# A two-product attention kernel: the second product turned round to 512 moving columns, with the running sum of the exponentials made by accumulating DMAs

## Chip, cores, metric

One core of one Trainium2 chip. The metric is the device time of one execution in microseconds (us), as the median of several runs. All runs told of here are of the fast state. A ratio is the mean time of one kernel's fast runs over the mean of the kernel before in the same rounds, so it is not quite the ratio of the medians that are quoted.

## The reference

Self-attention over 4 images of 64 x 64 positions, 256 channels, with 128-channel queries and keys, all in float32:

```python
q = x @ Wq + bq;  k = x @ Wk + bk;  v = x @ Wv + bv      # 4096 positions an image
pq, pk, pv = (t.reshape(B, -1, N) for t in (q, k, v))     # N = 4096: a reshape, not a transpose
energy = einsum('bcn,bcm->bnm', pq, pk)
attention = softmax(energy, axis=-1)
out = einsum('bcm,bnm->bcn', pv, attention).reshape(x.shape)
return gamma * out + x
```

## The kernel before

The energies of an image, 4096 x 4096, are never stored. For a group of queries the kernel walks over the keys in units: the first product (f32) gives energies in PSUM, ScalarE takes their exponentials, and the second product adds exponentials times v to accumulators. The second product keeps f32 accuracy from faster fp32r matmuls: each operand is given in three forms h, l and d (an upper part, the rest, and a difference), and three matmuls stand for one. A group has 256 queries, a unit has 4 key blocks of 128. The exponentials stand still as stationary operand, 128 queries at a time, and v's forms move. vh and vl carry two extra columns of ones, so that the softmax's denominator comes out of the same accumulation as column 256.

```python
NB = 256                                # queries a group; 64 groups, 8 units each
def energy(b, u):                       # first product, exp, upper part
    ...
    nc.tensor.matmul(sp[:, i, :], pr.pk[:, ...], pr.pqf[:, g * NB : (g + 1) * NB], ...)
    nc.scalar.activation(x[:, 2 * k : 2 * k + 2, :], sp, AF.Exp)
    ...
    nc.scalar.activation(h, x, AF.Identity, scale=UPPER)

def halves(b, u):                       # l = x - h, d = (1 + E) h - x, on VectorE
    ...

def attend(b, u):                       # second product, 24 matmuls a unit
    for j in range(NJ):                 # 2 halves of the queries
        a, bb = now["acc"][j]
        for i in range(4):
            for out_, left, right, ... in ((a, h, vh, ...), (a, l, vl, ...), (bb, d, vd, ...)):
                nc.tensor.matmul(out_, left[:, i, n], right[:, m, :], ...)

def finish(b, g, acc):                  # 1/z, combine a and bb, transpose back, add x, store
    ...

for u in range(STEPS):                  # the order on every engine's queue
    if u + LOOK < STEPS: energy(b, u + LOOK)      # LOOK = 2
    proceed()                           # one more piece of a finish that is under way
    if u + 1 < STEPS: halves(b, u + 1)
    attend(b, u)
    proceed()
```

Of the kernel before, what the change touches and what calls it, by code (L numbers as in the profile page):

```python
# [18 lines left out]
def kernel(  # L19
# [12 lines left out]

# [24 lines left out]
    P = 128  # L57
# [114 lines left out]

    NB = 256
    NJ = NB // P
    NG = N // NB
    NU = NM // 4
    STEPS = NG * NU
    LOOK = 2
    LAG = 3
# [7 lines left out]
    zall = const.tile([P, B * NG, NJ], F32, name="zall")  # L187
# [3 lines left out]
    with ExitStack() as fast:  # L191
# [5 lines left out]
        ppool, work = pool("ppool", 2), pool("work", 2)  # L197
# [4 lines left out]
        vh = qkv.tile([P, NM, C + 2], F32R, tag="vh", name="vh")  # L202
        vl = qkv.tile([P, NM, C + 2], F32R, tag="vl", name="vl")
        vd = qkv.tile([P, NM, C], F32R, tag="vd", name="vd")
        for t in (vh, vl):
            nc.vector.tensor_copy(t[:, :, C:], ones[:, : 2 * NM].rearrange("p (m t) -> p m t", t=2))

        images, units, now = [], {}, {}
# [11 lines left out]
        def image(b):  # L220
            def xt_out(i):
                return xtpool.tile([P, KC, 2, P], F32, tag="xt", name=f"xts_{b}_{i}")

            def v_out(i):
                now["v4"] = work.tile([P, KC, C], F32, tag="v4", name=f"v4_{b}_{i}")
                return now["v4"], bv4_sb, 1.0 / E

            images.append(Projection(b, xpool, qkv, (ps_s, "s"), xt_out, v_out))

        def project_v(b, i):  # L230
            images[b].v(i)
            v4 = now["v4"]
            m = slice(2 * i, 2 * i + 2)
            h = vh[:, m, :C]
            nc.scalar.activation(h, v4, AF.Identity, scale=UPPER * E)  # L235

            for t, f in ((vl, 1.0 / E), (vd, 1.0 / E + 1.0)):
                nc.vector.scalar_tensor_tensor(  # L238
                    t[:, m, :C], h.bitcast(F32), -f, v4, ALU.mult, ALU.add
                )  # L240

        def energy(b, u):

            g, t = divmod(u, NU)
            pr = images[b]
            x = ppool.tile([P, 4, NB], F32, tag="x", name=f"x_{b}_{u}")
            for k in range(2):
                sp = ps_s.tile([P, 2, NB], F32, tag="s", name=f"s_{b}_{u}_{k}")
                for i in range(2):
                    nc.tensor.matmul(  # L250
                        sp[:, i, :],
                        pr.pk[:, 4 * t + 2 * k + i, :],
                        pr.pqf[:, g * NB : (g + 1) * NB],
                        start=True,
                        stop=True,
                    )
                nc.scalar.activation(x[:, 2 * k : 2 * k + 2, :], sp, AF.Exp)  # L257
            h = ppool.tile([P, 4, NB], F32R, tag="h", name=f"h_{b}_{u}", bufs=LOOK + 1)
            nc.scalar.activation(h, x, AF.Identity, scale=UPPER)  # L259
            units[b, u] = x, h  # L260

        def halves(b, u):
            x, h = units[b, u]
            l = ppool.tile([P, 4, NB], F32R, tag="l", name=f"l_{b}_{u}")
            nc.vector.tensor_tensor(l, x, h.bitcast(F32), ALU.subtract)  # L265

            d = ppool.tile([P, 4, NB], F32R, tag="d", name=f"d_{b}_{u}")
# [3 lines left out]
            units[b, u] = h, l, d  # L271

        def attend(b, u):
            g, t = divmod(u, NU)
            if t == 0:
                now["acc"] = [
                    (
                        ps_o.tile([P, C + 2], F32, tag=f"a{j}", name=f"a{j}_{b}_{g}"),
                        ps_o.tile([P, C], F32, tag=f"b{j}", name=f"b{j}_{b}_{g}"),
                    )  # L280
                    for j in range(NJ)
                ]
            h, l, d = units[b, u]
            for j in range(NJ):
                a, bb = now["acc"][j]
                for i in range(4):
                    m = 4 * t + i
                    n = slice(j * P, (j + 1) * P)
                    for out_, left, right, first, last in (
                        (a, h, vh, True, False),  # L290
                        (a, l, vl, False, True),
                        (bb, d, vd, True, True),
                    ):
                        nc.tensor.matmul(  # L294
                            out_,
                            left[:, i, n],
                            right[:, m, :],
# [3 lines left out]
            if t == NU - 1:  # L301
                start(finish(b, g, now["acc"]))

        def finish(b, g, acc):
            xr = load_x(xpool, b, g)
            z = zall[:, b * NG + g, :]
            r = work.tile([P, 2, NJ], F32, tag="r", name=f"r_{b}_{g}")
            o = work.tile([P, NJ, C], F32, tag="o", name=f"o_{b}_{g}")
            for j in range(NJ):
                a, bb = acc[j]  # L310
                nc.vector.tensor_copy(z[:, j : j + 1], a[:, C : C + 1])
                nc.vector.reciprocal(r[:, 0, j : j + 1], z[:, j : j + 1])
                nc.vector.tensor_tensor(  # L313
                    r[:, 0, j : j + 1], r[:, 0, j : j + 1], gam, ALU.mult
                )
                nc.vector.tensor_scalar(
                    r[:, 1, j : j + 1], r[:, 0, j : j + 1], 1.0 + E, None, ALU.mult
                )
                nc.scalar.activation(  # L319
                    o[:, j, :], bb, AF.Identity, scale=r[:, 0, j : j + 1]  # L320
                )
                nc.vector.scalar_tensor_tensor(  # L322
                    o[:, j, :], a[:, :C], r[:, 1, j : j + 1], o[:, j, :], ALU.mult, ALU.add
                )
            yield
            yield
            tp = ps_s.tile([P, 2, NB], F32, tag="s", name=f"ot_{b}_{g}")
            for s in range(2):
                for j in range(NJ):
                    nc.tensor.transpose(  # L330
                        tp[:, s, j * P : (j + 1) * P], o[:, j, s * P : (s + 1) * P], ident
                    )
            nc.vector.tensor_tensor(xr, xr, tp, ALU.add)  # L333
            nc.gpsimd.dma_start(ov[b, g], xr)  # L334

        for b in range(B):
# [15 lines left out]
            halves(b, 0)  # L352
            for u in range(STEPS):
# [3 lines left out]
                if u + 1 < STEPS:  # L357
                    halves(b, u + 1)
# [7 lines left out]
    zf = zall.rearrange("p n j -> p (n j)")  # L366
    nc.vector.tensor_reduce(zs[:, 0:1], zf, AX.X, ALU.min)
    nc.vector.tensor_reduce(zs[:, 1:2], zf, AX.X, ALU.max)
    nc.vector.tensor_scalar(zs[:, 0:1], zs[:, 0:1], Z_LOW, None, ALU.is_lt)
    nc.vector.tensor_scalar(zs[:, 1:2], zs[:, 1:2], Z_HIGH, None, ALU.is_gt)  # L370
    nc.vector.tensor_tensor(zs[:, 0:1], zs[:, 0:1], zs[:, 1:2], ALU.add)
    with tc.tile_pool(name="ps_z", bufs=1, space=PSUM) as ps_z:
        zp = ps_z.tile([P, 1], F32, name="zp")
        nc.tensor.matmul(zp, ones, zs[:, 0:1], start=True, stop=True)
        nc.vector.tensor_copy(again, zp)

    NB = 512
    NG = N // NB
    NJ = NB // P
    NP = NM // 2  # L380
# [127 lines left out]
```

## Time and profile before

| | kernel before |
|---|---|
| median, range | 2666.5 us, 2664.6 to 2667.2 (3 runs) |
| TensorE, VectorE, ScalarE, GpSimd busy | 99%, 57%, 50%, 2% |
| granted TensorE clock | 0.999 |

The busy shares, the chain, the groups and the timeline of a group's end stand in the prediction below, with how to read them. Here is only what the waits of this kernel say (engine, line and tile that waited, for whom, us in total, times, longest):

```profile
ACT x L257 <- PE s L250: 1042.6, 880, 2.6
DVE l L265 <- issue: 841.8, 380, 2.6
PE a L294 <- DVE l L265: 1.9, 4, 0.5
```

ScalarE waits for TensorE's energies. VectorE waits too, with no other engine named (its buffers come free when TensorE is done with them). TensorE's own waits for VectorE are small: 1.9 us in the line above, and 3.0 us for d in the group lines of the prediction. The kernel is bound by TensorE.

### The profile page before, as it was taken

The page shows a single profiled execution, that of the slowest core. Times are in us where ns is not written, and L with a number is a line of the kernel's source. Part 1 is how long each engine was busy: PE and PEld are TensorE (multiplying, and loading weights), DVE is VectorE, ACT ScalarE, POOL GpSimd, SP SyncE. Part 2 cuts the span into 40 slices and gives each one's busy share as a digit, 9 for nine tenths or more (in the row PEclk, how much of TensorE's full clock was granted, in tenths as well). Part 3 has the DMA queues.
Part 4 walks back from the last instruction along what each step waited for, and adds up shares of the span by engine and source line. Part 5 has one row for each costly group of instructions (what it writes and reads, how often), then busy time and mean ns, then how long its engine had stood idle before and what let it go on. Part 6 is the DMA issues. An engine that isn't in the chain of part 4 may idle for free.

```text
span 2665.1 us, 42006 instructions
## 1 busy us (share of the span) xinstructions
PE 2639.4 (99%) x17922; PEld 2486.4 (93%) x17922; DVE 1506.8 (57%) x1993; ACT 1333.7 (50%) x1922; POOL 44.8 (2%) x70
## 2 busy tenths in 40 slices
PE   8999999999999999999999999999999999999998
PEld 7999999999899999999989999999998999999998
DVE  3555555555465555555545555555555555555555
ACT  3555555455455455455445555455545555545543
POOL 0000000000000000000000000000000000000000
PEclk9999999999999999999999999999999999999999
DMA  2000000000200000000020000000002000000000
GB/s 89 9 16 10 17 17 17 13 13 17 72 9 17 13 13 16 17 17 9 17 72 9 17 17 9 17 17 17 17 17 64 9 17 17 17 9 17 17 9 10
DMA packets 41667, 53.76 MB, mean 20 GB/s; under 512 B 3584, under 2 KB 37376, under 8 KB 41472
## 3 DMA queue, kind: packets, MB, share of 16 engines
q1 hardware_dynamic: 34816, 33.56, 4.1%
q0 software_dynamic: 5120, 16.78, 1.8%
q8 instruction: 142, 2.33, 0.3%
q10 hardware_dynamic: 1536, 0.66, 0.1%
q14 instruction: 53, 0.43, 0.0%
HBM read 34.21 MB, written 16.78 MB: 19 GB/s over the span
## 4 chain that ended last, share of the span: by engine, by line
PE 98%; DVE 1%; ACT 0%; DMA 0%; issue 0%; POOL 0%; ACTq 0%
PE a L294 37%; PE s L250 33%; PE b L294 18%; PE qk L136 4%; PE v L156 4%; PE ot L330 1%; PE xt L123 1%; DMA bv_sb<-in_L_conv_bv_dram 0%; DVE d L268 0%; DVE l L265 0%; ACT v L165 0%; ACT o L319 0%; DMA wqk_sb<-in_L_conv_Wk_dram 0%; DVE vl L238 0%; ACT vh L235 0%; DVE o L322 0%
## 5 line engine op out<-in xcount | busy, mean ns | idle before, releaser
L294 PE MATMUL a<-vh,h 128*128 128x258 f32 x4096 | 1242.3, 303 | 0.0
L294 PE MATMUL a<-vl,l 128*128 128x258 f32 x4096 | 1156.2, 282 | 1.9 <-DVE l L265 1.9
L294 PE MATMUL b<-vd,d 128*128 128x256 f32 x4096 | 1151.3, 281 | 3.0 <-DVE d L268 3.0
L257 ACT ACTIVATE x<-s 128x512 f32<-128x512 f32 x1024 | 610.5, 597 | 1056.2 <-PE s L250 1042.6
L265 DVE TENSOR_TENSOR l<-x,h 128x1024 fp32r<-128x1024 f32 x512 | 626.5, 1224 | 844.4 <-issue 841.8
L250 PE MATMUL s<-pq,pk 128*128 128x256 f32 x4096 | 966.5, 379 | 0.0
L250 PEld LDWEIGHTS s<-pq,pk 128*128 128x128 f32 x4096 | 741.2, 190 | 80.3
L294 PEld LDWEIGHTS a<-vl,l 128*128 128x128 f32 x4096 | 773.1, 189 | 14.5 <-DVE l L265 3.1
L294 PEld LDWEIGHTS a<-vh,h 128*128 128x128 f32 x4096 | 773.6, 189 | 11.5
L294 PEld LDWEIGHTS b<-vd,d 128*128 128x128 f32 x4096 | 774.0, 189 | 3.8 <-DVE d L268 3.8
L268 DVE SCALAR_TENSOR_TENSOR d<-h,x 128x1024 fp32r<-128x1024 f32 x512 | 623.9, 1219 | 0.0
L259 ACT ACTIVATE h<-x 128x1024 fp32r<-128x1024 f32 x512 | 542.7, 1060 | 16.3
L136 PE MATMUL qk<-wqk_sb,xts 128*128 128x256 f32 x512 | 123.5, 385 | 7.7 <-ACT xts L129 7.7
L156 PE MATMUL v<-xts,wv_sb 128*128 128x256 f32 x512 | 119.7, 379 | 0.0
L319 ACT ACTIVATE o<-b,r 128x256 f32<-128x256 f32 x128 | 60.6, 474 | 108.2 <-DVE r L313 108.2
L136 PEld LDWEIGHTS qk<-wqk_sb,xts 128*128 128x128 f32 x512 | 93.9, 193 | 19.4 <-ACT xts L129 8.8
L156 PEld LDWEIGHTS v<-xts,wv_sb 128*128 128x128 f32 x512 | 97.3, 190 | 13.2
L238 DVE SCALAR_TENSOR_TENSOR vl<-vh,v 128x512 fp32r<-128x512 f32 x64 | 44.4, 693 | 113.1 <-ACT vh L235 113.1
L165 ACT ACTIVATE v<-v,bv_sb 128x256 f32<-128x256 f32 x128 | 53.6, 469 | 105.6 <-PE v L156 105.6
L322 DVE SCALAR_TENSOR_TENSOR o<-a,r,o 128x256 f32<-128x256 f32 x128 | 62.0, 484 | 52.6 <-ACT o L319 52.6
L334 POOL DMA_DIRECT2D out_dram<-x x64 | 44.1, 690 | 2613.3 <-DVE x L333 2575.5
L333 DVE TENSOR_TENSOR x<-x,ot 128x512 f32<-128x512 f32 x64 | 44.0, 687 | 39.1 <-PE ot L330 39.1
(32 smaller groups left out, 406.1 us busy)
## 6 DMA issues: line engine op xcount, KB each, us to landing
x<-in_x_dram SPq DMA_DIRECT2D x128, 256.0 KB, 2.9
out_dram<-x POOLq DMA_DIRECT2D x64, 256.0 KB, 2.5
wv_sb<-in_L_conv_Wv_dram ACTq DMA_DIRECT2D x1, 256.0 KB, 4.4
wqk_sb<-in_L_conv_Wq_dram ACTq DMA_DIRECT2D x1, 128.0 KB, 2.1
wqk_sb<-in_L_conv_Wk_dram ACTq DMA_DIRECT2D x1, 128.0 KB, 3.1
bqk_sb<-in_L_conv_bq_dram ACTq DMA_DIRECT2D x1, 64.0 KB, 5.5
bqk_sb<-in_L_conv_bk_dram ACTq DMA_DIRECT2D x1, 64.0 KB, 5.8
bv_sb<-in_L_conv_bv_dram ACTq DMA_DIRECT2D x2, 0.5 KB, 5.1
```

The source lines that it names most:

```text
L136: nc.tensor.matmul(qk[:, s, :], self.xt[i][:, k, s, :], wqk_sb[:, k, :], start=(k == 0), stop=(k == KC - 1),)
L156: nc.tensor.matmul(vp[:, eh, :], wv_sb[:, k, eh * P : (eh + 1) * P], self.xt[i][:, k].rearrange("p s a -> p (s a)"), start=(k == 0), stop= ...
L165: nc.scalar.activation(to[:, eh, :], vp[:, eh, :], AF.Identity, bias=bias[:, eh : eh + 1], scale=scale,)
L238: nc.vector.scalar_tensor_tensor(t[:, m, :C], h.bitcast(F32), -f, v4, ALU.mult, ALU.add)
L250: nc.tensor.matmul(sp[:, i, :], pr.pk[:, 4 * t + 2 * k + i, :], pr.pqf[:, g * NB : (g + 1) * NB], start=True, stop=True,)
L257: nc.scalar.activation(x[:, 2 * k : 2 * k + 2, :], sp, AF.Exp)
L259: nc.scalar.activation(h, x, AF.Identity, scale=UPPER)
L265: nc.vector.tensor_tensor(l, x, h.bitcast(F32), ALU.subtract)
L268: nc.vector.scalar_tensor_tensor(d, h.bitcast(F32), 1.0 + E, x, ALU.mult, ALU.subtract)
L294: nc.tensor.matmul(out_, left[:, i, n], right[:, m, :], start=(m == 0 and first), stop=(m == NM - 1 and last),)
L319: nc.scalar.activation(o[:, j, :], bb, AF.Identity, scale=r[:, 0, j : j + 1])
L322: nc.vector.scalar_tensor_tensor(o[:, j, :], a[:, :C], r[:, 1, j : j + 1], o[:, j, :], ALU.mult, ALU.add)
```

## The change

The intent: let v's forms stand still and the exponentials move, 512 at a time, so that the number of second-product matmuls halves. The output then comes out with channels on partitions, which is the layout of the result, so the transposes at a group's end go. But a column sum of the exponentials is no longer a by-product: there are no columns of ones any more. It is made by DMAs that add each pair's exponentials to a tile in SBUF, off every engine's path, and at the group's end one f32 product with ones sums it over the partitions.

```diff
-    NB = 256
+    NB = 512            # 32 groups of 512 queries, 16 pairs of key blocks each
-    LAG = 3
+    LAG = 1
-        vh = qkv.tile([P, NM, C + 2], F32R, tag="vh", name="vh")      # likewise vl; vd without ones
+        vh, vl, vd = (qkv.tile([P, NM, C], F32R, ...) for f in "hld")
...
+        def forms(b, u):                # was halves(): l and d as before, and
+            if t == 0:
+                now["sum"] = work.tile([P, 2, NB], F32, tag="sum", ..., bufs=2)
+                nc.gpsimd.dma_start(now["sum"], x)
+            else:
+                nc.gpsimd.dma_start(now["sum"], x, accum_op=ALU.add)
...
         def attend(b, u):
-                        nc.tensor.matmul(out_, left[:, i, n], right[:, m, :], ...)
+                    for s in range(2):  # 12 matmuls a pair
+                        nc.tensor.matmul(to[s], left[:, m, s * P : (s + 1) * P], right[:, i, :], ...)
...
+        def finish(b, g, acc, total):   # in pieces; each yield is one proceed()
+            for s in range(2):
+                nc.scalar.copy(o[:, s, :], bb[s])
+                nc.vector.scalar_tensor_tensor(o[:, s, :], aa[s], 1.0 + E, o[:, s, :], ...)
+            yield
+            nc.vector.tensor_tensor(z, total[:, 0, :], total[:, 1, :], ALU.add)
+            yield
+            nc.tensor.matmul(zb, ones, z, start=True, stop=True)
+            nc.scalar.activation(z, zb, AF.Identity, accum_out=...)
+            yield
+            ...                         # two half reciprocals, scale by 1/z and gamma, add x, store
```

A unit is now a pair of key blocks with 512 queries: the same number of exponentials as a unit before. There are 512 units in both kernels. Not shown in the cut: x gets three buffers instead of two, x for the residual comes in two loads a group, and the check of the denominators' range at the end is written anew.

More of the change, by code (lines that the diff above doesn't have):

```diff
@@ L171, in v @@
                 )
-    NB = 256
-    NJ = NB // P
+    NB = 512
+    HB = NB // 2
     NG = N // NB
-    NU = NM // 4
-    STEPS = NG * NU
+    NP = NM // 2
+    STEPS = NG * NP
     LOOK = 2
-    LAG = 3
+    LAG = 1
     E = 2.0**-12
@@ L185 @@
     again = const.tile([P, 1], I32, name="again")
-    zall = const.tile([P, B * NG, NJ], F32, name="zall")
+    zsum = const.tile([P, 2, B * NG], F32, name="zsum")
     bv4_sb = const.tile([P, KC], F32, name="bv4_sb")
@@ L196 @@
         xpool, xtpool, qkv = pool("xpool", 4), pool("xtpool", LAG + 2), pool("qkv", 1)
-        ppool, work = pool("ppool", 2), pool("work", 2)
+        ppool, work = pool("ppool", 2), pool("work", 1)
         ps_s = pool("ps_s", 4, space=PSUM)
         ps_o = pool("ps_o", 1, space=PSUM)
-        vh = qkv.tile([P, NM, C + 2], F32R, tag="vh", name="vh")
-        vl = qkv.tile([P, NM, C + 2], F32R, tag="vl", name="vl")
-        vd = qkv.tile([P, NM, C], F32R, tag="vd", name="vd")
-        for t in (vh, vl):
-            nc.vector.tensor_copy(t[:, :, C:], ones[:, : 2 * NM].rearrange("p (m t) -> p m t", t=2))
-        images, units, now = [], {}, {}
+        vh, vl, vd = (
+            qkv.tile([P, NM, C], F32R, tag=f"v{f}", name=f"v{f}") for f in "hld"
+        )
+        images, pairs, now = [], {}, {}
         active = []
@@ L224, in v_out @@
             def v_out(i):
-                now["v4"] = work.tile([P, KC, C], F32, tag="v4", name=f"v4_{b}_{i}")
+                now["v4"] = work.tile([P, KC, C], F32, tag="v4", name=f"v4_{b}_{i}", bufs=2)
                 return now["v4"], bv4_sb, 1.0 / E
@@ L233, in project_v @@
             m = slice(2 * i, 2 * i + 2)
-            h = vh[:, m, :C]
+            h = vh[:, m, :]
             nc.scalar.activation(h, v4, AF.Identity, scale=UPPER * E)
@@ L238, in project_v @@
                 nc.vector.scalar_tensor_tensor(
-                    t[:, m, :C], h.bitcast(F32), -f, v4, ALU.mult, ALU.add
+                    t[:, m, :], h.bitcast(F32), -f, v4, ALU.mult, ALU.add
                 )
         def energy(b, u):
-            g, t = divmod(u, NU)
+            g, t = divmod(u, NP)
             pr = images[b]
-            x = ppool.tile([P, 4, NB], F32, tag="x", name=f"x_{b}_{u}")
-            for k in range(2):
-                sp = ps_s.tile([P, 2, NB], F32, tag="s", name=f"s_{b}_{u}_{k}")
-                for i in range(2):
-                    nc.tensor.matmul(
-                        sp[:, i, :],
-                        pr.pk[:, 4 * t + 2 * k + i, :],
-                        pr.pqf[:, g * NB : (g + 1) * NB],
-                        start=True,
-                        stop=True,
-                    )
-                nc.scalar.activation(x[:, 2 * k : 2 * k + 2, :], sp, AF.Exp)
-            h = ppool.tile([P, 4, NB], F32R, tag="h", name=f"h_{b}_{u}", bufs=LOOK + 1)
-            nc.scalar.activation(h, x, AF.Identity, scale=UPPER)
-            units[b, u] = x, h
-        def halves(b, u):
-            x, h = units[b, u]
-            l = ppool.tile([P, 4, NB], F32R, tag="l", name=f"l_{b}_{u}")
+            x = ppool.tile([P, 2, NB], F32, tag="x", name=f"x_{b}_{u}", bufs=LOOK + 1)
+            for i in range(2):
+                sp = ps_s.tile([P, NB], F32, tag="s", name=f"s_{b}_{u}_{i}")
+                nc.tensor.matmul(
+                    sp,
+                    pr.pk[:, 2 * t + i, :],
+                    pr.pqf[:, g * NB : (g + 1) * NB],
+                    start=True,
+                    stop=True,
+                )
+                nc.scalar.activation(x[:, i, :], sp, AF.Exp)
+            h = ppool.tile([P, 2, NB], F32R, tag="h", name=f"h_{b}_{u}", bufs=LOOK + 1)
+            nc.scalar.activation(h, x, AF.Identity, scale=UPPER)
+            pairs[b, u] = x, h
+        def forms(b, u):
+            g, t = divmod(u, NP)
+            x, h = pairs[b, u]
+            l = ppool.tile([P, 2, NB], F32R, tag="l", name=f"l_{b}_{u}")
             nc.vector.tensor_tensor(l, x, h.bitcast(F32), ALU.subtract)
-            d = ppool.tile([P, 4, NB], F32R, tag="d", name=f"d_{b}_{u}")
+            d = ppool.tile([P, 2, NB], F32R, tag="d", name=f"d_{b}_{u}")
             nc.vector.scalar_tensor_tensor(
@@ L270, in halves @@
             )
-            units[b, u] = h, l, d
+            if t == 0:
+                now["sum"] = work.tile([P, 2, NB], F32, tag="sum", name=f"sum_{b}_{g}", bufs=2)
+                nc.gpsimd.dma_start(now["sum"], x)
+            else:
+                nc.gpsimd.dma_start(now["sum"], x, accum_op=ALU.add)
+            if t == NP - 1:
+                now["last"] = now["sum"]
+            pairs[b, u] = h, l, d
         def attend(b, u):
-            g, t = divmod(u, NU)
+            g, t = divmod(u, NP)
             if t == 0:
                 now["acc"] = [
-                    (
-                        ps_o.tile([P, C + 2], F32, tag=f"a{j}", name=f"a{j}_{b}_{g}"),
-                        ps_o.tile([P, C], F32, tag=f"b{j}", name=f"b{j}_{b}_{g}"),
-                    )
-                    for j in range(NJ)
-                ]
-            h, l, d = units[b, u]
-            for j in range(NJ):
-                a, bb = now["acc"][j]
-                for i in range(4):
-                    m = 4 * t + i
-                    n = slice(j * P, (j + 1) * P)
-                    for out_, left, right, first, last in (
-                        (a, h, vh, True, False),
-                        (a, l, vl, False, True),
-                        (bb, d, vd, True, True),
-                    ):
+                    [
+                        ps_o.tile([P, NB], F32, tag=f"{k}{s}", name=f"{k}{s}_{b}_{g}")
+                        for s in range(2)
+                    ]
+                    for k in "ab"
+                ]
+            (h, l, d), (aa, bb) = pairs[b, u], now["acc"]
+            for i in range(2):
+                m = 2 * t + i
+                for to, left, right, first, last in (
+                    (aa, vh, h, True, False),
+                    (aa, vl, l, False, True),
+                    (bb, vd, d, True, True),
+                ):
+                    for s in range(2):
                         nc.tensor.matmul(
-                            out_,
-                            left[:, i, n],
-                            right[:, m, :],
+                            to[s],
+                            left[:, m, s * P : (s + 1) * P],
+                            right[:, i, :],
                             start=(m == 0 and first),
@@ L300, in attend @@
                         )
-            if t == NU - 1:
-                start(finish(b, g, now["acc"]))
-        def finish(b, g, acc):
-            xr = load_x(xpool, b, g)
-            z = zall[:, b * NG + g, :]
-            r = work.tile([P, 2, NJ], F32, tag="r", name=f"r_{b}_{g}")
-            o = work.tile([P, NJ, C], F32, tag="o", name=f"o_{b}_{g}")
-            for j in range(NJ):
-                a, bb = acc[j]
-                nc.vector.tensor_copy(z[:, j : j + 1], a[:, C : C + 1])
-                nc.vector.reciprocal(r[:, 0, j : j + 1], z[:, j : j + 1])
-                nc.vector.tensor_tensor(
-                    r[:, 0, j : j + 1], r[:, 0, j : j + 1], gam, ALU.mult
-                )
-                nc.vector.tensor_scalar(
-                    r[:, 1, j : j + 1], r[:, 0, j : j + 1], 1.0 + E, None, ALU.mult
-                )
-                nc.scalar.activation(
-                    o[:, j, :], bb, AF.Identity, scale=r[:, 0, j : j + 1]
-                )
-                nc.vector.scalar_tensor_tensor(
-                    o[:, j, :], a[:, :C], r[:, 1, j : j + 1], o[:, j, :], ALU.mult, ALU.add
-                )
+            if t == NP - 1:
+                start(finish(b, g, now["acc"], now["last"]))
@@ new lines, in finish @@
+        def finish(b, g, acc, total):
+            n = b * NG + g
+            aa, bb = acc
+            o = work.tile([P, 2, NB], F32, tag="o", name=f"o_{b}_{g}")
+            for s in range(2):
+                nc.scalar.copy(o[:, s, :], bb[s])
+                nc.vector.scalar_tensor_tensor(
+                    o[:, s, :], aa[s], 1.0 + E, o[:, s, :], ALU.mult, ALU.add
+                )
+            xr = []
+            for f in range(2):
+                t = xpool.tile([P, 2, XB], F32, tag="x", name=f"xr_{b}_{g}_{f}")
+                nc.sync.dma_start(t, xv[b, 2 * g + f])
+                xr.append(t)
@@ L325, in finish @@
             yield
+            z = work.tile([P, NB], F32, tag="z", name=f"z_{b}_{g}")
+            nc.vector.tensor_tensor(z, total[:, 0, :], total[:, 1, :], ALU.add)
             yield
-            tp = ps_s.tile([P, 2, NB], F32, tag="s", name=f"ot_{b}_{g}")
-            for s in range(2):
-                for j in range(NJ):
-                    nc.tensor.transpose(
-                        tp[:, s, j * P : (j + 1) * P], o[:, j, s * P : (s + 1) * P], ident
-                    )
-            nc.vector.tensor_tensor(xr, xr, tp, ALU.add)
@@ L334, in finish @@
-            nc.gpsimd.dma_start(ov[b, g], xr)
+            zb = ps_s.tile([P, NB], F32, tag="s", name=f"zb_{b}_{g}")
+            nc.tensor.matmul(zb, ones, z, start=True, stop=True)
+            nc.scalar.activation(z, zb, AF.Identity, accum_out=zsum[:, 0, n : n + 1])
+            yield
+            for f in range(2):
+                half = z[:, f * HB : (f + 1) * HB]
+                nc.vector.reciprocal(half, half)
+                yield
+            t = work.tile([P, NB], F32, tag="v4", name=f"t_{b}_{g}", bufs=2)
@@ new lines, in finish @@
+            nc.scalar.activation(t, z, AF.Identity, accum_out=zsum[:, 1, n : n + 1])
+            for f in range(2):
+                of = o[:, :, f * HB : (f + 1) * HB]
+                rb = z[:, f * HB : (f + 1) * HB].unsqueeze(1).to_broadcast([P, 2, HB])
+                nc.vector.scalar_tensor_tensor(of, of, gam, rb, ALU.mult, ALU.mult)
+                yield
+                nc.vector.tensor_tensor(xr[f], xr[f], of, ALU.add)
+                nc.gpsimd.dma_start(ov[b, 2 * g + f], xr[f])
+                yield
@@ L351 @@
                 energy(b, u)
-            halves(b, 0)
+            forms(b, 0)
             for u in range(STEPS):
@@ L357 @@
                 if u + 1 < STEPS:
-                    halves(b, u + 1)
+                    forms(b, u + 1)
                 attend(b, u)
@@ L365 @@
     zs = const.tile([P, 2], F32, name="zs")
-    zf = zall.rearrange("p n j -> p (n j)")
-    nc.vector.tensor_reduce(zs[:, 0:1], zf, AX.X, ALU.min)
-    nc.vector.tensor_reduce(zs[:, 1:2], zf, AX.X, ALU.max)
-    nc.vector.tensor_scalar(zs[:, 0:1], zs[:, 0:1], Z_LOW, None, ALU.is_lt)
-    nc.vector.tensor_scalar(zs[:, 1:2], zs[:, 1:2], Z_HIGH, None, ALU.is_gt)
-    nc.vector.tensor_tensor(zs[:, 0:1], zs[:, 0:1], zs[:, 1:2], ALU.add)
-    with tc.tile_pool(name="ps_z", bufs=1, space=PSUM) as ps_z:
-        zp = ps_z.tile([P, 1], F32, name="zp")
-        nc.tensor.matmul(zp, ones, zs[:, 0:1], start=True, stop=True)
-        nc.vector.tensor_copy(again, zp)
-    NB = 512
-    NG = N // NB
+    nc.vector.tensor_reduce(zs, zsum, AX.X, ALU.max)
+    nc.vector.tensor_scalar(zs[:, 0:1], zs[:, 0:1], Z_HIGH, None, ALU.is_gt)
+    nc.vector.tensor_scalar(zs[:, 1:2], zs[:, 1:2], 1.0 / Z_LOW, None, ALU.is_gt)
+    nc.vector.tensor_tensor(again, zs[:, 0:1], zs[:, 1:2], ALU.add)
     NJ = NB // P
-    NP = NM // 2
     xg, og = columns(x, NB), columns(out, NB)
```

## The prediction

> **What bounds the kernel now.** I read the page's busy shares and the chain that ended last first, then the costliest groups, then the timeline of one end of a query group, then the waits and the DMA records.
>
> ```profile
> PE 2639.4 (99%) x17922; PEld 2486.4 (93%) x17922; DVE 1506.8 (57%) x1993; ACT 1333.7 (50%) x1922; POOL 44.8 (2%) x70
> PE 98%; DVE 1%; ACT 0%; DMA 0%; issue 0%; POOL 0%; ACTq 0%
> L294 PE MATMUL a<-vh,h 128*128 128x258 f32 x4096 | 1242.3, 303 | 0.0
> L294 PE MATMUL b<-vd,d 128*128 128x256 f32 x4096 | 1151.3, 281 | 3.0 <-DVE d L268 3.0
> L250 PE MATMUL s<-pq,pk 128*128 128x256 f32 x4096 | 966.5, 379 | 0.0
> L265 DVE TENSOR_TENSOR l<-x,h 128x1024 fp32r<-128x1024 f32 x512 | 626.5, 1224 | 844.4 <-issue 841.8
> L268 DVE SCALAR_TENSOR_TENSOR d<-h,x 128x1024 fp32r<-128x1024 f32 x512 | 623.9, 1219 | 0.0
> ```
>
> TensorE is on the chain for 98% of the span and almost never waits, so the time is its instruction count times its pace. The means in the groups (281 to 303 ns) are latencies of pipelined instructions and not the pace; the pace is the distance between starts:
>
> ```profile
> 1000.98 0.28 PE L294 MATMUL b<-vd,d 128*128 128x256 f32 x1
> 1001.09 0.28 PE L294 MATMUL a<-vh,h 128*128 128x258 f32 x1
> 1001.21 0.28 PE L294 MATMUL a<-vl,l 128*128 128x258 f32 x1
> 1001.26 0.49 DVE L322 SCALAR_TENSOR_TENSOR o<-a,r,o 128x256 f32<-128x256 f32 x1 [0.41 <-ACT o L319]
> 1001.33 0.28 PE L294 MATMUL b<-vd,d 128*128 128x256 f32 x1
> 1001.33 1.60 PEld L250 LDWEIGHTS s<-pq,pk 128*128 128x128 f32 x8
> 1001.45 1.89 PE L250 MATMUL s<-pq,pk 128*128 128x256 f32 x8
> ...
> 1003.17 0.72 PE L330 MATMUL ot<-ident,o 128*128 128x128 f32 x4
> ```
>
> A matmul of the second product starts 0.12 us after the one before it (119.4 ns as the mean over the whole trace, scattering from 113 to 129). The eight records of the first product take 1.72 us from their start to the next instruction, 215.7 ns each with almost no scatter. An f32 product of 256 columns shows as two records (4096 records for 2048 calls), each streaming twice the cycles; the fp32r products show as one.
>
> So a unit (512 of them) costs 24 x 119.4 + 8 x 215.7 = 2.866 + 1.726 = 4.59 us, together 2351 us. The 64 group ends have four transposes at some 153 ns, 0.61 us each, 39 us. The remaining 2665 - 2351 - 39 = 275 us are four projections, the start and the tail.
>
> **What the Trainium skill says.** (1) "TensorE: Matmul & The Clock Gate", section "Wait — 56ns, not 53.3ns?": a warm matmul of N columns follows the last one after N / 2.4 GHz plus about 2.5 ns. For 512 array cycles that is 215.8 ns, which the first product meets (215.7). For 256 it is 109.2, for 258 110; the second product's 119.4 is about 10 ns over it. (2) Same page, section "LDWEIGHTS (loading the stationary operand)": a load takes its column count / 1.2 GHz, 107 ns for 128 columns. In the second product every matmul has its own load, as the equal counts of PE and PEld show, and a load of 107 ns has hardly any room beside 109 ns of streaming; beside 215 ns, in the first product, it is invisible. I take the 10 ns for that. (3) "DMA: Bandwidth & Descriptors", sections "Two DMAs through the same engine are not ordered" and "Rules for kernel authors": an accumulating DMA reads its destination and writes it later, so each must wait for the semaphore of the one before. The built program does wait for it on the issuing queue. No run shows its price yet. (4) "Collectives: The Full Stack", section "The bandwidth ceiling: the fold count and why AG ≠ RS ≠ AR": an add inside a DMA reads two sources per byte written and so runs at about half the rate of a copy. Nothing in the trace before accumulates, so it neither agrees nor disagrees.
>
> **The change, part by part.**
> 1. Second product. 12288 matmuls with 256 or 258 columns become 6144 with 512. Columns shrink only from 3.162 to 3.146 million; what goes is half the weight loads and per-matmul cost. If the load hides, a matmul takes what 512 array cycles take in this trace, 215.7 ns: 12 x 215.7 = 2.588 us a unit against 2.866, so -0.278 us x 512 = -142 us.
> 2. First product: half as many records, each of 1024 cycles, 1024 / 2.4 + 2.4 = 429 ns. 4 x 429 = 1.716 against 1.726 us: -5 us.
> 3. Group ends. The transposes go, -39 us. In their place come 32 f32 products with ones (2 x 429 ns, 27 us), placed on TensorE's queue directly after the next energies and before the next second product. They wait for the column sum z, which the vector queue makes after both accumulator evictions. From the last matmul: copy of b0 on ACT (128x512 from PSUM, 573 ns as the transposes' copies), two evictions of a on DVE (128x512 with a PSUM source was 687 ns; I take 700), z (690 ns): 0.57 + 0.7 + 0.7 + 0.7 = 2.7 us. TensorE has 1.72 us of energies meanwhile, so it idles about 1.0 us, x 32 = 32 us. Sum of this part: -39 + 27 + 32 = +20 us.
> 4. Ends. The last group's chain (z, ones product, reciprocals, two scaled adds, store) is longer than the old one: +7 us. Loads of x at an image's start find two free buffers and not four, while residual tiles hold the others: I allow +1.5 us an image, 5 us.
> 5. ACT keeps its work (2 x 597 + 1060 ns a unit). DVE gets per group evictions, z, reciprocals of 2 x 256 elements (not measured here beyond one element; at 8 cycles an element an estimate is 2 x 2.1 us), and four passes of 0.69 us: some 9 us per 16 units, 0.6 us a unit on top of 2.44, or 70% of the new unit. The forms are made a unit ahead, so this hides.
>
> With the DMAs hidden: 2665 - 142 - 5 + 20 + 12 = **about 2550 us**, and 2555 to 2560 with small losses at the boundaries. A unit then takes 2.59 + 1.72 = 4.31 us.
>
> 6. The sum. 512 DMAs of 512 KB, SBUF to SBUF, of which 480 add and wait for the landing of the one before (each group's first is a copy). This must keep pace with 4.31 us. The nearest measured thing is the store:
>
> ```profile
> out_dram<-x POOLq DMA_DIRECT2D x64, 256.0 KB, 2.5
> L334 POOL DMA_DIRECT2D out_dram<-x x64 | 44.1, 690 | 2613.3 <-DVE x L333 2575.5 <-DVE l L265 37.9
> ```
>
> Its packet records: the first packet starts 1.26 us after the issue, each engine moves four packets of 4 KB at 188 ns (21.8 GB/s), landing is at 2.5 us. So 1.75 us is fixed and 0.75 us is data; the semaphore-to-issue step is another 0.29 us in the timeline. 512 KB as a plain copy: 1.75 + 0.29 + 8 x 0.188 = 3.5 us, which would hide. With two reads per write: at the rate above 1.75 + 0.29 + 3.0 = 5.0 us; at the 31 GB/s per engine of the collectives page, 4.15 us. The bound of 4.31 lies inside this bracket. Three x buffers let the chain run up to two units behind, which smooths but doesn't raise the rate.
>
> **The rivals.**
> A. *The DMA chain becomes the bound.* Then a unit takes T and not 4.31 us, and each 0.1 us of T above it costs 512 x 0.1 = 51 us: T of 4.5 gives about 2660 (no change), 5.0 about 2910, 6 about 3400. For it: the serial wait, the double read, the 1.75 us that no transfer size removes, and two stores a group that sit in the same in-order GpSimd queue. Against it: SBUF to SBUF has no DRAM on either side, so fixed part and rate may both be better than the store's; the DMA engines are nearly idle now; and the new kernel splits its reciprocals and final passes into small pieces, which only pays where the pace is so close to TensorE's that DVE matters.
> B. *The 10 ns is not a hidden load but a cost per matmul or per column.* Per matmul, 512 columns take 213.3 + 12.7 = 226 ns, half the gain goes and the time is about 2615. Per column they take 2 x 118.4 = 237 ns, and the time is about 2680. For it: 258 columns seem 1 to 2 ns slower than 256. Against it: streaming a column at a fixed rate would not scatter by 15 ns, while the first product does not scatter at all.
> C. *The wait for z grows* because the last accumulation lands late. If the chain keeps up, it is one or two units ahead and z does not feel it; if not, this is part of A.
>
> **Range and chances.** I give "DMA hidden" 0.6 and A 0.4. Hidden, the time is 2540 to 2625, near 2560, mostly over 2% faster (2% is 2613), with B's worse forms leaving a tenth of it within 2%. Under A about a fifth lands still faster by 2% or near it, a quarter within 2%, the rest slower, with a tail to 3000 and beyond. That makes faster 0.55, same 0.16, slower 0.29. The predicted time of 2585 is the hidden case with an allowance for A and B; the range is 2540 to 2880.
>
> **What would show it.** Starts of second-product matmuls 216 ns apart: part 1 right; 226 or 237: rival B. TensorE's gap ahead of the ones product of about 1 us, released by DVE z: part 3. Issue to landing of the accumulating DMA below 4 us with TensorE on the chain for 95%: A is wrong. Exponentials on ACT waiting for DMA landings, DMA or GpSimd high in the chain, and a unit longer than 4.4 us: A is right, and the prediction falls by 51 us for each 0.1 us. DVE waits ahead of L294's counterpart would show that part 5 was taken too lightly.

## The result, and the profile after

| | before | after |
|---|---|---|
| median | 2666.8 us (4 runs) | 2840.4 us (4 runs, 2836.2 to 2842.4) |
| ratio | | 1.065, 95% interval 1.063 to 1.067: slower |
| TensorE busy | 99% | 93% |
| granted TensorE clock | 0.999 | 0.971 |

The page of the changed kernel, with the lines that answer to those of before (busy shares, chain, groups, DMA issues; the last column of the issues is the median from issue to landing in us):

```profile
PE 2643.5 (93%) x9536; PEld 1802.1 (64%) x9536; DVE 1582.5 (56%) x1573; ACT 1325.9 (47%) x1986; POOL 475.2 (17%) x582
PE 41%; DMA 28%; issue 7%; ACT 3%; DVE 1%; POOLq 0%; ACTq 0%; POOL 0%
L246 PE MATMUL s<-pq,pk 128*128 128x512 f32 x2048 | 960.5, 591 | 0.0
L274 POOL DMA_DIRECT2D sum<-x x480 | 410.6, 855 | 1929.0 <-DMA sum<-x 1313.6
L298 PE MATMUL b<-d,vd 128*128 128x512 f32 x2048 | 639.7, 394 | 3.0 <-DVE d L267 3.0
L327 PE MATMUL zb<-z,ones 128*128 128x512 f32 x64 | 57.6, 998 | 158.5 <-DVE z L324 158.5
sum<-x POOLq DMA_DIRECT2D x512, 512.0 KB, 4.5
```

The chain that ended last was 98% TensorE. Now the DMAs of the sum, which did not exist before, are its second largest part, with 28%. TensorE is still 93% busy, and that number hides the matter: a busy engine on a longer span. Its one large wait, 158.5 us, is ahead of the ones product, 32 times in all. The waits say where it comes from:

```profile
POOL sum L274 <- DMA sum<-x: 1313.6, 319, 5.6
ACT x L253 <- DMA sum<-x: 568.0, 206, 4.4
PE zb L327 <- DVE z L324: 158.5, 32, 8.9
```

GpSimd waits for the last accumulation before it issues the next. ScalarE waits for the DMA before it may write new exponentials over x. A stretch of the timeline in the middle of an image shows the step:

```profile
1000.75 1.09 ACT L253 ACTIVATE x<-s 128x512 f32<-128x512 f32 x2 [2.85 <-DMA sum<-x]
1001.17 0.85 POOL L274 DMA_DIRECT2D sum<-x  x1 [4.19 <-DMA sum<-x]
...
1002.74 1.88 PE L246 MATMUL s<-pq,pk 128*128 128x512 f32 x4
...
1005.83 1.09 ACT L253 ACTIVATE x<-s 128x512 f32<-128x512 f32 x2 [2.90 <-DMA sum<-x]
1006.25 0.85 POOL L274 DMA_DIRECT2D sum<-x  x1 [4.23 <-DMA sum<-x]
...
1007.23 1.88 PE L246 MATMUL s<-pq,pk 128*128 128x512 f32 x4
```

From issue to issue the accumulation takes 1006.25 - 1001.17 = 5.08 us (median over the trace 5.06). TensorE's unit, from energies to energies, takes 1007.23 - 1002.74 = 4.49 us. The buffers let TensorE run ahead inside a group. At the group's end it stands at the ones product, because z needs the last accumulation. The clock then pays too:

```profile
394.25 2.04 PE L327 MATMUL zb<-z,ones 128*128 128x512 f32 x2 [4.78 <-DVE z L324]
395.31 1.84 PE L298 MATMUL a<-h,vh 128*128 128x512 f32 x2
396.95 0.82 PE L298 MATMUL a<-l,vl 128*128 128x512 f32 x2
397.60 0.62 PE L298 MATMUL b<-d,vd 128*128 128x512 f32 x2
398.06 0.62 PE L298 MATMUL a<-h,vh 128*128 128x512 f32 x2
```

After 4.78 us of idling the two matmuls that start at 395.31 take 1.64 us until the next pair (at the same place one unit later it is 0.87). Two that start at 397.60 take 0.46 again. In the trace's clock records TensorE has half its clock after 28 of the 32 gaps, mostly for 3.4 or 6.8 us, hence the mean of 0.971. The four gaps without such a stretch are 2.8 to 3.2 us long; every gap of 3.38 us or more has one. What the half clock costs in time by itself was not measured.

The account, by group: issues of the sum span 78.5 us from a group's first to its last, and the next group's first, which waits for no earlier sum, follows 0.5 us later. 32 x 79 = 2530 us, and some 305 us of projections, start and tail make the 2834 us of the span. Fifteen steps of 5.06 us would be 75.9 us: the first step of a group takes 5.84 us in the median and the fourth and fifth 5.5 and 5.7, because landing takes 5.0 to 5.3 us there and not 4.5. Other transfers are under way then (the last addition of the group before, the residual's loads and the stores); that they are the reason was not tested.

### The profile page after: what moved, and what is told of

Same layout as the page of the kernel before. It is cut to its first block, busy times and chain, and to the rows that moved or that the text cites. A ratio compares the mean times of both kernels' runs of the same rounds, so it can differ in the third digit from the quotient of the medians.

```text
span 2834.3 us, 25712 instructions
## 1 busy us (share of the span) xinstructions
PE 2643.5 (93%) x9536; PEld 1802.1 (64%) x9536; DVE 1582.5 (56%) x1573; ACT 1325.9 (47%) x1986; POOL 475.2 (17%) x582
## 4 chain that ended last, share of the span: by engine, by line
PE 41%; DMA 28%; issue 7%; ACT 3%; DVE 1%; POOLq 0%; ACTq 0%; POOL 0%
DMA sum<-x 28%; PE a L298 14%; PE s L246 12%; PE b L298 7%; PE v L155 3%; PE qk L135 3%; ACT h L255 2%; PE zb L327 2%; ACT x L253 1%; PE xt L122 1%; DVE z L324 1%; DVE l L264 0%; DVE d L267 0%; ACT v L164 0%; POOLq L274 0%
## 5 line engine op out<-in xcount | busy, mean ns | idle before, releaser
L246 PE MATMUL s<-pq,pk 128*128 128x512 f32 x2048 | 960.5, 591 | 0.0
L298 PE MATMUL a<-h,vh 128*128 128x512 f32 x2048 | 865.1, 504 | 1.1 <-ACT h L255 1.1
L274 POOL DMA_DIRECT2D sum<-x x480 | 410.6, 855 | 1929.0 <-DMA sum<-x 1313.6
L298 PE MATMUL a<-l,vl 128*128 128x512 f32 x2048 | 654.0, 401 | 1.8 <-DVE l L264 1.7
L298 PE MATMUL b<-d,vd 128*128 128x512 f32 x2048 | 639.7, 394 | 3.0 <-DVE d L267 3.0
L298 PEld LDWEIGHTS a<-h,vh 128*128 128x128 f32 x2048 | 396.6, 194 | 297.7 <-issue 245.0
L246 PEld LDWEIGHTS s<-pq,pk 128*128 128x128 f32 x2048 | 385.4, 188 | 287.7 <-issue 237.0
L298 PEld LDWEIGHTS a<-l,vl 128*128 128x128 f32 x2048 | 392.7, 192 | 98.2 <-DVE l L264 4.8
L298 PEld LDWEIGHTS b<-d,vd 128*128 128x128 f32 x2048 | 389.3, 190 | 101.6 <-DVE d L267 7.3
L327 PE MATMUL zb<-z,ones 128*128 128x512 f32 x64 | 57.6, 998 | 158.5 <-DVE z L324 158.5
L333 DVE RECIPROCAL z<-z 128x256 f32<-128x256 f32 x64 | 108.0, 1725 | 15.8 <-ACT z L328 15.7
```

Of the source, the lines that this page charges most:

```text
L246: nc.tensor.matmul(sp, pr.pk[:, 2 * t + i, :], pr.pqf[:, g * NB : (g + 1) * NB], start=True, stop=True,)
L274: nc.gpsimd.dma_start(now["sum"], x, accum_op=ALU.add)
L298: nc.tensor.matmul(to[s], left[:, m, s * P : (s + 1) * P], right[:, i, :], start=(m == 0 and first), stop=(m == NM - 1 and last),)
L327: nc.tensor.matmul(zb, ones, z, start=True, stop=True)
L333: nc.vector.reciprocal(half, half)
```

## The experiments

| run | median, us | ratio to before in its rounds | result |
|---|---|---|---|
| e1_no_sum | 2639.9 | 0.990 | wrong |
| e2_copies | 2642.2 | 0.991 | wrong |
| e3_halves | 2639.1 | 0.990 | right |
| e4_halves_late | 2615.1 | 0.981 (0.979 to 0.982) | right |
| e5_late_only | 2834.9 | 1.064 | right |
| e6_split256 | 2669.8 | 1.001 | right |
| e7_bf16 | 2522.2 | 0.946 (0.944 to 0.947) | accepted by the comparison with the reference |
| e8_dve_sum | 2614.6 | 0.981 (0.979 to 0.983) | right |
| e9_half_load | 2614.6 | 0.981 | wrong |

The first four and the next four each shared a chip and the runs of the kernel before (2666.1 and 2666.6 us); e9_half_load had its own (2666.1 us).

**The theory after the result** was the prediction's rival A: the serial chain of accumulating DMAs sets the pace. Its own rivals: TensorE or the place of the ones product does, whatever the DMAs do; and, inside the chain, the DMA engines' bandwidth instead of one step's latency.

### e1_no_sum: the chain taken away

```diff
             if t == 0:
                 now["sum"] = work.tile(...)
                 nc.gpsimd.dma_start(now["sum"], x)
-            else:
-                nc.gpsimd.dma_start(now["sum"], x, accum_op=ALU.add)
```

> Only the first DMA of each group is kept, the 480 accumulating ones are gone; the result is wrong on purpose. Theory A (the serial chain of accumulating DMAs, 5.05 us from issue to issue, sets the pace): the time falls to TensorE's own, 512 units of 12 x 231 + 4 x 429 ns = 4.49 us, 32 group ends of about 1.9 us, 280 us of projections and ends, about 2640 us (2620 to 2660). If the DMA traffic also slows the second product's matmuls (231 ns apart where I predicted 216), their spacing falls towards 216 and the time towards 2560. Rival B (TensorE's place for the ones product and the vector work ahead of z, whatever the DMAs do): the gap of 5.4 us ahead of the ones product stays and the time stays over 2780.

Measured 2639.9 us, where theory A said about 2640, with 97% of the chain on TensorE. So the chain costs 200 us, and what is left is TensorE's pace. The second product's spacing is the same 231 ns (mean over the trace) with and without the DMA traffic, so the DMAs don't slow TensorE's streaming. The run also says that even with the chain gone the change is worth 1%, and not the 4% that my sum gave.

### e2_copies: the same chain, without the addition

```diff
-                nc.gpsimd.dma_start(now["sum"], x, accum_op=ALU.add)
+                nc.gpsimd.dma_start(now["sum"], x)
```

> The 480 accumulating DMAs become plain copies of the same 512 KB to the same tile, each still waiting for the one before; the result is wrong on purpose. If the second read of the addition is what makes the chain too slow, issue to issue falls from 5.05 to 5.05 - 8 x (335 - 187) ns = about 3.9 us, under the unit's 4.49, and the time is that of the run without DMAs within 1%. If the wait alone does it (fixed part), issue to issue stays over 4.5 us and the time over 2700.

Measured 2642.2 us: the serial wait alone does no harm. GpSimd's timeline shows the step where it is not held up by x (the last note names ScalarE, but that issue came 0.54 us after the landing of the copy before, as do those that the profile puts down to the DMA):

```profile
536.05 0.55 POOL L272 DMA_DIRECT2D sum<-x  x1 [0.16 <-issue]
539.70 0.53 POOL L272 DMA_DIRECT2D sum<-x  x1 [3.10 <-issue]
543.14 0.53 POOL L272 DMA_DIRECT2D sum<-x  x1 [2.91 <-ACT h L255]
```

A copy's step takes 3.44 us (539.70 to 543.14) and not the 3.9 that I expected, an addition's 5.06. The difference of 1.6 us has two parts. In the packet records a 4 KB packet takes 157 ns on its engine in the copy and some 336 ns in the addition, which over the eight packets of each engine makes 2.76 us from first packet to last instead of 1.44. And the issuing instruction itself takes 0.85 us and not 0.53. The packets alone decide it: 5.06 - 0.32 is still over 4.49, 5.06 - 1.32 is not. So the addition, not the wait, lifts the step over the 4.49 us of a unit. (A copy lacks both the second read and the adding; the run does not tell them apart.)

### e3_halves: two chains of half the size

```diff
-                nc.gpsimd.dma_start(now["sum"], x)
-            else:
-                nc.gpsimd.dma_start(now["sum"], x, accum_op=ALU.add)
+            how = {"accum_op": ALU.add} if t else {}
+            for i in range(2):
+                nc.gpsimd.dma_start(now["sum"][:, i, :], x[:, i, :], **how)
```

> Each accumulating DMA is split in two of 256 KB, one for each half of the sum: two chains that don't wait for each other; the result stays right. Theory A, latency and not bandwidth: the data of a unit takes 8 x 335 ns = 2.7 us, a half's chain about 3.7 to 4.2 us a step, so both hide under 4.49 us and the time is 2640 to 2680. If the DMA engines' bandwidth for additions were the bound, nothing changes: 2840. If the GpSimd queue with twice the issues binds (2 x 0.85 us a unit), it does not show either, since 1.7 is under 4.49.

Measured 2639.1 us with a right result and the full number of added bytes: as fast as no additions at all. The page's share and issue lines:

```profile
PE 97%; ACT 1%; DVE 1%; DMA 0%; issue 0%; POOL 0%; ACTq 0%
sum<-x POOLq DMA_DIRECT2D x1024, 256.0 KB, 3.3
```

A half lands 3.3 us after its issue and not 4.5, and two of them are under way at once. The queue's packets take 59% of the 16 engines' time and not 51%. So it was the latency of one serial step and not bandwidth.

TensorE still waits ahead of the ones product, as the prediction said it would with the DMAs hidden:

```profile
298.45 1.88 PE L246 MATMUL s<-pq,pk 128*128 128x512 f32 x4
301.07 1.10 PE L327 MATMUL zb<-z,ones 128*128 128x512 f32 x2 [0.75 <-ACT x L253]
```

Four energy records of 429 ns end their streaming at 298.45 + 1.72 = 300.17; the ones product starts 0.90 us later. I had put it at 1.0. The note names ScalarE's exponential, which ended at 300.96; z ended at 300.92, within 0.04 us of it. That the product waits for z, and not for the exponential, is read from the program: the PSUM buffer that it takes held energies of a unit earlier, which were read by then.

### e4_halves_late: the ones product behind the next second product

```diff
             nc.vector.tensor_tensor(z, total[:, 0, :], total[:, 1, :], ALU.add)
             yield
+            yield
             zb = ps_s.tile(...)
             nc.tensor.matmul(zb, ones, z, start=True, stop=True)
```

> As the split chains, and the ones product is put half a unit later on TensorE's queue, behind the next second product instead of ahead of it, so that z is ready when it comes. If TensorE idles about 1 us a group end for z when the chain keeps up: 30 us less than the split chains alone, about 2610 to 2640, and no gap ahead of the ones product. If a part of the gap comes from elsewhere, or half-clock stretches follow each gap, the gain is larger, up to 60 us.

Measured 2615.1 us, 24 us less than e3_halves; 28 gaps of 0.9 us are 25. In its trace TensorE waits ahead of the ones product only once, for 2.4 us. This version is 1.9% under the kernel before, clear of the noise; whether it is 2% is unclear, as the interval just reaches that.

### e5_late_only: the same move with the chain left whole

The edit is that of e4_halves_late, on the unsplit DMAs.

> The changed kernel with its unsplit accumulating DMAs, and only the ones product put behind the next second product; the result stays right. If the serial chain alone sets the time, little is gained: 15 steps of 5.05 us and one of 0.5 us a group stay, about 2790 to 2830. If a good part of the 174 us over the split version is TensorE standing before the ones product while the next exponentials can't be started (the chain then idles too), more comes back: 2700 to 2770.

Measured 2834.9 us (ratio 1.064, against 1.065 for the change itself): nothing gained, and 5 us over my bracket of 2790 to 2830. The wait has only moved:

```profile
POOL sum L274 <- DMA sum<-x: 1486.3, 347, 5.9
ACT x L253 <- DMA sum<-x: 836.5, 293, 4.5
PE a L298 <- DVE o L314: 118.7, 28, 5.9
```

TensorE no longer waits for z but for the accumulators, which are evicted late: ScalarE's copy of b stands in its queue behind exponentials that wait for the DMA (3.6 us at one group's end in the trace), and VectorE's eviction waits for that copy (3.9 us there). And GpSimd's and ScalarE's waits for the DMAs grew. So the 158 us ahead of the ones product were a symptom of the chain; the place of the ones product on TensorE costs what e4_halves_late gave, 24 us, and only when the chain keeps up.

### e6_split256: the 512 columns undone

```diff
-                        nc.tensor.matmul(to[s], left[...], right[:, i, :], start=(m == 0 and first), ...)
+                        for c in (slice(0, HB), slice(HB, NB)):
+                            nc.tensor.matmul(to[s][:, c], left[...], right[:, i, c],
+                                start=(m == 0 and first and c.start == 0), ...)
```

(The start flag goes to the first half only.)

> The best version so far with each second-product matmul of 512 columns cut into two of 256 columns with the same stationary operand: 24 a unit as in the kernel before; the result stays right. This undoes the 512 columns alone. If a matmul's time is that of the kernel before (119 ns), a unit gets 24 x 119 - 12 x 231 = 84 to 94 ns longer: +43 to +48 us, about 2660. If the spacing depends on the operand that stands still and not on the column count, it differs from 119 and the time from 2660 by over 15 us.

Measured 2669.8 us: 55 us more than e4_halves_late, where I expected 43 to 48, and as slow as the kernel before. TensorE's timeline (each row four matmuls):

```profile
1002.44 0.64 PE L299 MATMUL a<-l,vl 128*128 128x256 f32 x4
1002.92 0.64 PE L299 MATMUL b<-d,vd 128*128 128x256 f32 x4
```

Four take 0.48 us: the spacing is 120 ns, as in the kernel before, though now v stands still and the exponentials move. So the spacing does not depend on which operand moves, but on cutting 512 columns in two. In the trace each half has its own weight load (15680 loads for 15680 matmul records), so the run undoes the halved number of matmuls and of loads together. With that, the 512 columns are the whole of the change's gain: 24 x 120 - 12 x 231 = 108 ns a unit, 55 us.

### e7_bf16: the operands' type

```diff
-F32R = mybir.dt.float32r
+F32R = mybir.dt.bfloat16        # and h.bitcast(F32) becomes h
```

> The best version so far with the six operands of the second product in bf16 and not fp32r: too coarse, so the result may be wrong on purpose. It asks why 512 columns take 231 ns and not the 216 that the f32 products need for 512 cycles. If that is a matter of the fp32r operands (their loads or their streaming), the spacing is 216 and the time 2615 - 512 x 12 x 15 ns = 2523 (2500 to 2540). If it is the accumulation into two banks in turn, or the issue of load and matmul, the spacing stays 226 to 236 and the time 2590 to 2620.

Measured 2522.2 us. TensorE's timeline (each row two matmuls):

```profile
1000.57 0.59 PE L298 MATMUL a<-h,vh 128*128 128x512 bf16 x2
1001.00 0.59 PE L298 MATMUL a<-l,vl 128*128 128x512 bf16 x2
1001.43 0.59 PE L298 MATMUL b<-d,vd 128*128 128x512 bf16 x2
```

Two take 0.43 us, 216 each, without scatter. The same program with fp32r needs 231, scattering from 224 to 236. So the 15 ns belong to the fp32r operands, not to issue or accumulation, which are alike in both. Whether to their streaming or their loads this run leaves open, as the records of the loads become shorter too (98 ns instead of 188). (The three forms were made for fp32r; the comparison with the reference accepts the bf16 result, but how much accuracy it costs was not measured, so I don't put it forward as the better kernel.)

### e8_dve_sum: the sum on VectorE

```diff
-                nc.gpsimd.dma_start(now["sum"], x, accum_op=ALU.add)
+                nc.vector.tensor_tensor(now["sum"], now["sum"], x, ALU.add)
```

with the ones product late as in e4_halves_late (and a VectorE copy for a group's first pair).

> No DMAs for the sum: VectorE adds each pair of exponentials to the running sum itself (one more pass of 1.22 us a unit), ones product late; the result stays right. VectorE then has 2.44 + 1.22 + about 0.6 us a unit, 4.26 of 4.49 us. If that still hides, 2615 to 2640, as with split DMAs; if its bursts at group ends can't be hidden any more, TensorE waits for l and d and the time is 2660 to 2750. It tells whether the DMAs were needed at all.

Measured 2614.6 us, the same as with split DMAs:

```profile
PE 2582.8 (99%) x9536; PEld 1771.0 (68%) x9536; DVE 2123.4 (81%) x2085; ACT 1354.2 (52%) x1986; POOL 44.8 (2%) x70
L274 DVE TENSOR_TENSOR sum<-sum,x 128x1024 f32<-128x1024 f32 x480 | 584.1, 1217 | 0.0
```

VectorE takes the 584 us of additions and is 81% busy, and TensorE does not feel it. The accumulating DMAs saved an engine that had room.

### e9_half_load: half the weight load

```diff
+                    w = P if m in (0, NM - 1) else P // 2
-                        nc.tensor.matmul(to[s], left[:, m, s * P : (s + 1) * P], right[:, i, :], ...)
+                        nc.tensor.matmul(to[s][:w, :], left[:, m, s * P : s * P + w], right[:, i, :], ...)
```

> The best fp32r version so far (split DMAs, ones product late), but in all key blocks except the first and last the stationary operand of the second product has 64 columns and not 128, so that each load is half as long while 512 columns still move; half the output channels are wrong on purpose. If the 15 ns that an fp32r matmul of 512 columns takes over 216 are a load that isn't wholly hidden, the spacing falls to 216 to 224 and the time to 2525 to 2570. If the cost lies in the streaming of the moving fp32r columns, the spacing stays at 224 to 236 and the time at 2615 (2600 to 2625).

Measured 2614.6 us, spacing 224 to 239 ns, mean 230 (231 in e4_halves_late): no change of note.

```profile
L299 PEld LDWEIGHTS a<-h,vh 128*64 128x64 f32 (+1 forms) x2048 | 284.5, 139 | 367.9 <-issue 252.7
```

The load fell from 189 ns in e4_halves_late to 139 in this group's mean (134 for the loads of 64 columns), and the matmuls hardly noticed. The idea behind the prediction's largest term, a weight load that does not quite hide, is refuted at 512 columns. At 256 columns it was not tested.

## Why the prediction was wrong

It forecast a gain of 3% and the kernel lost 6.5%, though the range of 2540 to 2880 holds the result. By its steps:

- **Part 6 and rival A, the sum: the step that failed.** The prediction took it that one accumulation would be hidden under TensorE's unit; it takes 5.06 us where a unit takes 4.49. The upper end of its bracket was 5.0 us; the copy was put at 3.5 us and measured 3.44 in e2_copies. That both come so close is partly luck. Data took 2.76 us and not 3.0 in the addition (1.44 and not 1.5 in the copy), while from landing to the next issue it took 0.53 us and not 0.29, which was the time after a VectorE instruction. The choice between the ends was wrong. I gave "hidden" 0.6 on the lower end (4.15 us, an estimate from the 31 GB/s per engine of "Collectives: The Full Stack", section "The bandwidth ceiling: the fold count and why AG ≠ RS ≠ AR") and on the look of the code, where the trace's own rate had already given a step longer than the 4.31 us of a unit. Counting two reads, the reading side runs at 2 x 4096 B in 336 ns, 24 GB/s per engine. e1, e2 and e3 settle it: without the additions, with copies in their place, or with two independent chains, the 200 us are gone.
- **Rival A's size.** "5.0 about 2910" was too much, because each group's first DMA waits for no earlier one: of 16 steps a group one takes 0.5 us, and 32 x 4.5 us = 144 us are saved against 16 full ones. Against that, a group's other 15 steps took 78.5 us and not 15 x 5.0 = 75. The rest of the distance was not taken apart.
- **Part 1, the second product: right in kind, mis-sized.** 6144 matmuls were to take 216 ns and take 231: 12 x 15 = 180 ns a unit, 92 us in all. That is the whole distance from the 2555 us of the hidden case to the 2640 of e1_no_sum, within 8 us. Its reason fell with it. The 10 ns over the rule were taken for a weight load; e9_half_load shows no effect of the load's length at 512 columns, and e7_bf16 shows that the surplus comes with fp32r. Rival B's "per matmul" gives 226 and its "per column" 237; the measured 120 and 231 lie between, and 0.43 ns a column plus 9 ns fits both (two terms for two points, so no test). What in the hardware makes fp32r so stays open.
- **Part 2** was right: 429 ns a record.
- **Part 3, the group ends:** right. A gap of 0.90 us against 1.0, and 24 us for moving the ones product against 32.
- **Part 4,** the ends: not measured by itself.
- **Part 5:** right in its conclusion; VectorE hides even the additions (e8_dve_sum). The two reciprocals of a group were put at 2.1 us each and took 1.73.
- **Rival C**, that a longer wait for z is only a part of A, was right: in e5_late_only that wait moves elsewhere and nothing is gained.

So the account of the loss is: 2667 before; -55 for 512 columns instead of 256; +28 for the group ends and the rest of the restructuring (the remainder; the starts of the energies in the traces give some 23 of it, as a unit with a group's end is 1.84 us longer than another in e3_halves, 32 times, and was 0.56 us longer before, 64 times), which gives the 2640 of e1_no_sum and e3_halves; +200 for a chain whose step of 5.06 us is longer than the 4.49 us that TensorE takes for a unit.

## What to carry to other kernels

Work that is moved to DMAs is free only if its longest serial step is shorter than the pace of the loop it feeds: add up issue, data, landing and wait for one step before asking about bandwidth, and where the step is too long, split it into chains that don't wait for each other. When an estimate's bracket straddles the bound, as here, the end that comes from the trace's own rates deserves more weight than the one from elsewhere. And before an engine is relieved at any cost, look whether it had room: VectorE did the sum at no cost in time.

## What the Trainium skill lacked or had wrong

- "TensorE: Matmul & The Clock Gate", section "Wait — 56ns, not 53.3ns?": N / 2.4 GHz plus 2.5 ns holds for f32 (215.7 and 429 ns for 512 and 1024 cycles) and bf16 (216 ns for 512 columns), but not for fp32r, which no page gives a pace for: 119 to 120 ns for 256 columns, 231 for 512.
- Same page, section "LDWEIGHTS (loading the stationary operand)": its time of column count / 1.2 GHz is not contradicted (a load's record fell by 54 ns, from 188 to 134, with 64 columns fewer; the rule gives 53), but the surplus is not named there, and the load does not explain it: with 64 columns instead of 128 the spacing stayed at 230 ns.
- "DMA: Bandwidth & Descriptors" has no time for an accumulating DMA. Here 512 KB within SBUF take 4.5 us from issue to landing (a copy 2.9), 5.06 us from issue to dependent issue (a copy 3.44), some 336 ns a packet of 4 KB (a copy 157), and GpSimd 0.85 us to issue (a copy 0.53).
- "Collectives: The Full Stack", section "The bandwidth ceiling: the fold count and why AG ≠ RS ≠ AR": that an add runs at half a copy's rate agrees (336 / 157 = 2.1); its 31 GB/s per engine does not carry over, 24 GB/s were read.
- "VectorE: DVE Perf Modes", section "First, the fixed hardware budget", names a repeat count of 8 for the reciprocal and no time. I read it as 8 cycles an element in my estimate; a 128x256 reciprocal took 1.73 us, at most 6.5 cycles an element at the page's 0.96 GHz, and not 2.1 us.
